# Transposes in pairs ahead of the scores: a two-layer graph-attention kernel

## The chip, the cores and the metric

The kernel runs on one core of a Trainium2 chip. A core has five engines that this text calls by short names: PE (TensorE, matrix products), DVE (VectorE), ACT (ScalarE), POOL (GpSimd) and SP (SyncE, which issues DMAs). PE multiplies with a grid of 128 x 128 cells, reads its operands from the on-chip memory SBUF and writes its results to PSUM, a small memory from which DVE or ACT must fetch them. The metric is the device time of one execution in microseconds (us).

## What is computed

The input x is 16 graphs ("batches") of 1,024 nodes with 256 features, adj a 1024 x 1024 mask for each graph. Two layers follow each other, both as `x = x + layer(relu(layernorm(x)))`. Cut to what matters:

```python
def _L0_gnn_ref(x, adj_matrix, gamma1, beta1, gamma2, beta2, W1, b1, W2, b2):   # layer 0
    normed = layer_norm(x, gamma1, beta1)
    qkv = normed.reshape(b_, n_, H, HD).transpose(0, 2, 1, 3)     # 8 heads of 32; q = k = v
    scores = jnp.einsum('bhqd,bhkd->bhqk', qkv, qkv) * scale
    attn = jax.nn.softmax(jnp.where(mask, scores, -jnp.inf), axis=-1)
    out = jnp.einsum('bhqk,bhkd->bhqd', attn, qkv)
    x = x + out.transpose(0, 2, 1, 3).reshape(b_, n_, d_)
    y = layer_norm(x, gamma2, beta2)
    return x + jax.nn.gelu(y @ W1 + b1, approximate=False) @ W2 + b2

def _L1_gnn_ref(feat, adj, W, a_1, a_2, a_12, W_1, W_2):          # layer 1
    h = feat @ W
    logits = swapaxes(h @ a_1) + h @ a_2 + (h @ a_12) @ swapaxes(h)
    e = where(adj > 0, leaky_relu(logits, 0.2), NEG_INF)
    h_prime = softmax(e) @ feat
    return elu(feat @ W_1 + h_prime @ W_2)
```

All products are in float32.

## The kernel before

**Two kinds of work share PE.** Layer 0's attention is cut into *units*: for a batch, 2 halves of the queries x 2 groups of 4 heads x 8 key tiles give 32 units. A unit (`attention`, `scores` at line 922, `weigh` at 969) computes the scores of 4 heads into PSUM (tile `s`, L937), DVE adds the mask (L958), ACT takes Exp (L961), and a unit later PE weighs the values with it (tile `o`, L974). The sums of the softmax are made by DMA: POOL issues for each key tile two transfers that add `e` to `acc` (L999), and two units after a group's end PE reduces `acc` to `den` (L888); `finish` (L901) transposes `ds` and `os` and divides.

Everything else of a batch (the MLP of layer 0 and all of layer 1) is the generator `rest` (L1054). It runs one batch behind: between two units of batch b + 1, PE does some pieces of `rest` of batch b. A batch is handled in 4 chunks of 256 nodes:

- `prepare(c)` (L1039): statistics on DVE (`norm_stats`, L699, with a power on POOL, L710), later the normalized rows y; `turn(c)` (L1085) transposes them on PE (pty, L1095), and DVE scales them into yT (L1099);
- `expand(c)` (ph, hid) and `contract(c)` (po, L1149 adds it to xb): the two products of the MLP;
- `prepare1(c)`, `turn1(c)` (L1155, L1165): normalized rows ft, transposes ptf, Relu on ACT into fT (L1174);
- `project` (puT, to uT by ACT, L1186), `values` (pg, to gw by ACT or DVE in turn, L1201), `weights` (lg, then L1219, L1224 on DVE, Exp on ACT, L1225), and `attend` (own part pf, copied to z by ACT at L1240, and pa).

The next batch's values `va` are prepared by `prologue` (L740), whose `turn(i)` (L783) transposes them for chunk i (ptk, L788) into kT.

**The order** is written out: a loop takes the generators by a number that each yields as its place, so that the pieces of `rest` are spread evenly over the units, and the instructions of each engine keep the order in which the loop issued them. A transpose is not issued where it is asked for: `ask(turn, c)` puts it in the list `turns`, and `make_turns` (L872) issues what is in it just ahead of the next unit's scores. `wait_for` lets `rest` go on only when a turn has been made. `defer(us, f)` (L723) issues f when an estimated clock has run on by so many us, or earlier if `run_deferred` forces it.

**PE's shapes.** A product of `rest` is issued as four products of 32 columns (`matmul`, L565; "128*32" in the profile), scores use 32 rows ("32*128"), and a transpose the whole grid ("128*128"). A group is four transposes of 128 x 128 into one PSUM tile.

**PSUM.** Two tiles hold the scores, one the weighed values; all else shares three tiles (pool `psm`, `ps_tile`, L558). A new tile takes the place of the one that was let go first, and PE waits until that has been read.

In a steady batch there are 16 groups of transposes ahead of scores: four each of pty, ptf and ptk, and four pairs of ptds and ptos from `finish`; a pair stands in one place and is counted once here.

Of the kernel before, what the change touches and what calls it, by code (L numbers as in the profile page):

```python
# [493 lines left out]
def fast_path(  # L494
# [63 lines left out]
    def ps_tile(shape, name, dtype=F32):  # L558
        return psm.tile(shape, dtype, tag="ps", name=name)
# [15 lines left out]
    def rows(src, b, t, cols=slice(None)):  # L575
        pair = src[b, t // 2 * 2 * P : (t // 2 + 1) * 2 * P, cols]
        return pair.rearrange("(p r) d -> p r d", r=2)[:, t % 2, :]
# [121 lines left out]
    def norm_stats(srcs, name):  # L699

        nt = len(srcs)
        st = smallp.tile([P, nt, nc.vector.BN_STATS_DIM], F32, tag="st", name=f"st_{name}")
        mv = smallp.tile([P, nt, nc.vector.BN_AGGR_DIM], F32, tag="mv", name=f"mv_{name}")
        for t in range(nt):
            nc.vector.bn_stats(st[:, t, :], srcs[t])
            nc.vector.bn_aggr(mv[:, t, :], st[:, t, :])
        ve = smallp.tile([P, nt], F32, tag="ve", name=f"ve_{name}")
        nc.vector.tensor_scalar_add(ve, mv[:, :, 1], EPS)
        rs = smallp.tile([P, nt], F32, tag="rs", name=f"rs_{name}")
        nc.gpsimd.tensor_tensor(rs, ve, mhalf[:, :nt], op=ALU.pow)  # L710
        return mv, rs

    def normalize(dst, src, mv, rs, t):
        nc.vector.tensor_scalar(
            dst, src, mv[:, t, 0:1], rs[:, t : t + 1], op0=ALU.subtract, op1=ALU.mult
        )
# [6 lines left out]
    def defer(us, f):  # L723
        deferred.append((clock[0] + us, len(deferred), f))

        return clock[0] + us
# [13 lines left out]
    def prologue(b, st):  # L740
# [42 lines left out]
        def turn(i):  # L783
            clock[0] += 0.5
            pt = ps_tile([P, NG, CW], f"ptk_{b}_{i}")
            for g in range(NG):
                for j in range(TPC):
                    nc.tensor.transpose(  # L788
                        pt[:, g, j * P : (j + 1) * P], va[:, i * TPC + j, g * P : (g + 1) * P], ident
                    )  # L790
            nc.scalar.copy(kT[:, :, i * CW : (i + 1) * CW], pt)
# [5 lines left out]
            lambda i: measure(i, "b"),  # L797
            value,
            lambda i: None,
            lambda i: turns.append((1, lambda: turn(i))),  # L800
        ]
        if b == 0:

# [64 lines left out]
    turns = []  # L868
# [170 lines left out]
    def prepare(b, st, c):  # L1039

        h = hs[b]
        assert finished[b, c // 2] == NG
        ts = range(c * TPC, (c + 1) * TPC)
        mv, rs = norm_stats([h[t // TPH][:, t % TPH, :] for t in ts], f"c{b}_{c}")

        def apply():
            y = tmpp.tile([P, TPC, D], F32, tag="y", name=f"y_{b}_{c}")
            for i, t in enumerate(ts):
                normalize(y[:, i, :], h[t // TPH][:, t % TPH, :], mv, rs, i)
            st["y", c] = y, None  # L1050

        st["y", c] = None, defer(5.0, apply)

    def rest(b, st, tails):  # L1054
# [4 lines left out]
        def load(c):  # L1059
            for t in range(c * TPC, (c + 1) * TPC):  # L1060
                xt.append(xbp.tile([P, D], F32, tag="xb", name=f"xb_{b}_{t}"))
                nc.sync.dma_start(xt[t], rows(x, b, t))


        def add_residuals(t):
            ht = h[t // TPH][:, t % TPH, :]
            nc.gpsimd.tensor_add(ht, ht, b2r)
            nc.gpsimd.tensor_add(xt[t], xt[t], ht)
# [4 lines left out]
        def ask(turn, c):  # L1073

            def f():
                clock[0] += 0.5
                turn(c)
                turned.add((turn, c))
            turns.append((1, f))

        def wait_for(turn, c):
            while (turn, c) not in turned:
                yield 0.0, None

        def turn(c):  # L1085
            if st["y", c][1] is not None:
                run_deferred(st["y", c][1])
            y = st["y", c][0]
            for i in range(TPC):
                defer(4.0 * i + 2.0, lambda t=c * TPC + i: add_residuals(t))  # L1090
            yT[c] = tmpp.tile([P, DC, CW], F32, tag="yT", name=f"yT_{b}_{c}")
            pt = ps_tile([P, DC, CW], f"pty_{b}_{c}")
            for dc in range(DC):
                for i in range(TPC):
                    nc.tensor.transpose(  # L1095
                        pt[:, dc, i * P : (i + 1) * P], y[:, i, dc * P : (dc + 1) * P], ident
                    )
            for dc in range(DC):
                nc.vector.tensor_scalar(  # L1099
                    yT[c][:, dc, :],  # L1100
                    pt[:, dc, :],
                    g2[:, dc : dc + 1],
                    be2[:, dc : dc + 1],
                    op0=ALU.mult,
                    op1=ALU.add,
                )

        def expand(c):
            yield from wait_for(turn, c)
            hid = midp.tile([P, FC, CW], F32, tag="mid", name=f"hid_{b}_{c}")  # L1110
            for f0 in range(0, FC, 2):
                ph = ps_tile([P, 2, CW], f"ph_{b}_{c}_{f0}")
                for i in range(2):
                    for dc in range(DC):
                        matmul(
                            ph[:, i, :],
                            w1[:, dc, (f0 + i) * P : (f0 + i + 1) * P],
                            yT[c][:, dc, :],
                            start=(dc == 0),
                            stop=(dc == DC - 1),  # L1120
                        )
                nc.vector.tensor_tensor(  # L1122
                    hid[:, f0 : f0 + 2, :],
                    ph,
                    b1c[:, f0 : f0 + 2].unsqueeze(2).to_broadcast([P, 2, CW]),
                    op=ALU.add,
                )
                yield 1.75, True
            return hid, defer(1.0, lambda: nc.scalar.activation(hid, hid, AF.Gelu))  # L1129

        def contract(c, hid):
            hid, ready = hid
            run_deferred(ready)
            for i in range(TPC):
                t = c * TPC + i
                po = ps_tile([P, D], f"po_{b}_{t}")
                for f in range(FC):
                    matmul(
                        po,
                        hid[:, f, i * P : (i + 1) * P],  # L1140
                        w2[:, f, :],
                        start=(f == 0),
                        stop=(f == FC - 1),
                    )
                    if f == FC // 2 - 1:
                        open_sums[0] = 1
                        yield 1.75, True
                        open_sums[0] = 0
                nc.vector.tensor_add(xt[t], po, xt[t])  # L1149
                yield 1.75, True  # L1150
# [124 lines left out]
            yield 1.75, True  # L1275

        load(0)
        ask(turn, 0)
        yield
        load(1)  # L1280
        hid = {0: (yield from expand(0))}
        ask(turn, 1)
        yield from tails[b]()
        while finished.get((b, 1), 0) < NG:
            yield 0.0, None
        prepare(b, st, 2)
        load(2)
        hid[1] = yield from expand(1)
        ask(turn, 2)
        prepare(b, st, 3)  # L1290
        yield from contract(0, hid[0])
        load(3)
        hid[2] = yield from expand(2)
        ask(turn, 3)
        prepare1(0)
        yield from contract(1, hid[1])
        hid[3] = yield from expand(3)
        prepare1(1)
        fT = st["fT"] = midp.tile([P, DC, N], F32, tag="mid", name=f"fT_{b}")
        ask(turn1, 0)  # L1300
        yield from contract(2, hid[2])
        prepare1(2)
        ask(turn1, 1)
        yield from contract(3, hid[3])
        uT = midp.tile([P, DC, N], F32, tag="mid", name=f"uT_{b}")
        prepare1(3)
        ask(turn1, 2)

        def some_values(*ts):
            for t in ts:  # L1310
                values(t, fT)
                yield 0.9, t % 2 == 1
# [5 lines left out]
        def some_weights(c, *pairs):  # L1318
            for i in pairs:
                first.append(weights(c, i))  # L1320
                yield 1.75, True
# [3 lines left out]
        yield from wait_for(turn1, 1)  # L1325
        yield from project_half(0, 0)
        yield from some_values(0, 1)
        ask(turn1, 3)
        yield from project_half(0, 1)
        yield from some_values(2, 3)  # L1330
        yield from wait_for(turn1, 2)
        yield from some_values(4, 5)
        yield from some_weights(0, 0, 1)
        yield from wait_for(turn1, 3)
        yield from project_half(1, 0)
        yield from project_half(1, 1)
        yield from some_values(6, 7)

        before = None
        for c in range(NCH):  # L1340
# [81 lines left out]
    while any(p is not None for p in places):  # L1422
        i = min((p, i) for i, p in enumerate(places) if p is not None)[1]
# [101 lines left out]
```

## Time and profile before

| | |
|---|---|
| median of 4 runs | 3539.82 us (3533.82 to 3546.57) |
| profiled execution | 3545.33 us, span of its instructions 3543.5 us |
| busy: PE, DVE, ACT, POOL | 98%, 77%, 52%, 40% of the span |
| granted clock of PE, mean | 0.997 |
| one batch, from its scores to the next batch's | some 217 us (ptf of the first chunk at 447.82, 667.02, 881.32, ... us) |
| transposes: ptk, ptds, pty, ptf, ptos | 256 instructions each, 272 to 273 ns a piece in the median |
| mask add on DVE (L958), 128 x 1024 | 1217 ns |
| Exp of scores on ACT (L961), 128 x 1024 | 1058 ns |
| acc DMAs: 864 of 512 KB | 6.0 us from issue to landing (median), the queue's packets take 69.9% of 16 DMA engines |

In the profile, a line such as `L1171 PE MATMUL ptf<-ident,ft` names the line of the code, the engine, the operation, and the tiles written and read. In lists by time the first number is the start in us from the span's start, the second the length of a run of equal instructions, and in brackets stands an idle time before it with what ended it. An end of a matmul is modelled, so costs on PE are best read from start to start. A wait "PE ptf L1171 <- DVE ft L714" means that PE's instruction writing ptf was held up until DVE had written ft.

### The profile page before, as it was taken

To read this page: it belongs to the slowest core of one execution; us is meant where nothing else is said; L and a number is where in the kernel's file an instruction comes from. 1 tells how busy PE (TensorE), PEld (TensorE's weight loads), DVE (VectorE), ACT (ScalarE), POOL (GpSimd) and SP (SyncE) were. 2 spreads that over 40 slices of the span, in tenths; PEclk is the share of its full clock that TensorE was granted. 3 is DMA by queue.
4 is the path that set the end of the run, shared out by engine and by line. 5 is a ranking of instruction groups with operands and counts; after the bars stand their busy time and mean duration, and the time that the engine had idled before them with its cause. 6 is when DMAs were issued, how large, how long until landed. Compare 5 with 4: busy or idle time off the path is not lost.

```text
span 3543.5 us, 107149 instructions
## 1 busy us (share of the span) xinstructions
PE 3455.9 (98%) x46494; PEld 1679.0 (47%) x46494; DVE 2737.4 (77%) x5189; ACT 1855.0 (52%) x2184; POOL 1417.8 (40%) x1708
## 2 busy tenths in 40 slices
PE   6999999999999999999999999999999999999998
PEld 2344444444444444444444444544444444444477
DVE  6878787787777878878887887887878777787744
ACT  5655554555555555555555555455555555555522
POOL 3543443434434344453434434344443444433220
PEclk9999999999999999999999999999999999999999
DMA  7788989999899998989999898998989989899710
GB/s 184 159 175 175 186 167 175 172 187 186 158 178 171 182 191 164 186 169 182 190 170 187 167 188 175 179 183 162 186 165 187 183 164 181 165 182 181 151 41 14
DMA packets 281859, 597.79 MB, mean 169 GB/s; under 512 B 94882, under 2 KB 130084, under 8 KB 281380
## 3 DMA queue, kind: packets, MB, share of 16 engines
q0 software_dynamic: 124416, 453.04, 69.9%
q1 hardware_dynamic: 154276, 134.41, 15.0%
q8 instruction: 367, 6.01, 0.7%
q10 hardware_dynamic: 2688, 3.41, 0.3%
q14 instruction: 112, 0.92, 0.1%
HBM read 104.21 MB, written 16.78 MB: 34 GB/s over the span
## 4 chain that ended last, share of the span: by engine, by line
PE 72%; DMA 14%; issue 5%; DVE 4%; POOL 2%; ACT 2%; ACTq 0%; SPq 0%; POOLq 0%; DVEq 0%
DMA acc<-e 13%; PE s L937 12%; PE pa L570 10%; PE o L974 10%; PE lg L570 9%; PE ph L570 8%; PE po L570 7%; PE pf L570 3%; PE pg L570 2%; PE puT L570 2%; DVE e L958 1%; PE den L888 1%; PE ptk L788 1%; PE pa L567 1%; POOL acc L999 1%
## 5 line engine op out<-in xcount | busy, mean ns | idle before, releaser
L999 POOL DMA_DIRECT2D acc<-e x864 | 762.7, 889 | 1669.0 <-DMA acc<-e 678.5
L961 ACT ACTIVATE e<-e 128x1024 f32<-128x1024 f32 x852 | 895.9, 1058 | 1011.5 <-DVE e L958 773.2
L958 DVE TENSOR_TENSOR e<-s,mk 128x1024 f32<-128x1024 f32 x852 | 1002.7, 1217 | 178.8 <-PE s L937 149.4
L937 PE MATMUL s<-kT 32*128 32x512 f32 x4096 | 595.7, 643 | 7.6 <-DVE e L958 5.3
L974 PE MATMUL o<-e,va 128*32 128x512 f32 x3456 | 463.8, 607 | 2.1 <-ACT e L961 2.1
L570 PE MATMUL lg<-fT,uT 128*32 128x256 f32 x7680 | 449.2, 380 | 0.0
L570 PE MATMUL ph<-yT,w 128*32 128x256 f32 x7808 | 447.4, 379 | 0.0
L570 PE MATMUL pa<-gw,e 128*32 128x258 f32 x7552 | 446.6, 380 | 0.0
L570 PE MATMUL po<-w,hid 128*32 128x256 f32 x7680 | 439.0, 379 | 0.0
L570 PEld LDWEIGHTS ph<-yT,w 128*32 128x32 f32 x7808 | 255.2, 110 | 212.3 <-issue 51.1
L570 PEld LDWEIGHTS lg<-fT,uT 128*32 128x32 f32 x7680 | 252.6, 110 | 209.3 <-issue 44.7
L570 PEld LDWEIGHTS po<-w,hid 128*32 128x32 f32 x7680 | 249.8, 110 | 209.4 <-issue 59.5
L570 PEld LDWEIGHTS pa<-gw,e 128*32 128x32 f32 x7552 | 244.9, 110 | 210.1 <-issue 56.9
L1219 DVE SCALAR_TENSOR_TENSOR e<-lg,gw,mk 128x256 f32<-128x256 f32 x512 | 223.2, 477 | 73.5 <-PE lg L570 63.0
L1225 ACT ACTIVATE e<-e,shift 128x512 f32<-128x512 f32 x256 | 182.1, 717 | 178.9 <-DVE e L1224 118.3
L1122 DVE TENSOR_TENSOR hid<-ph,b1c 128x512 f32<-128x512 f32 x256 | 175.2, 687 | 93.2 <-PE ph L570 77.6
L937 PEld LDWEIGHTS s<-kT 32*128 32x128 f32 x4096 | 163.8, 183 | 169.3 <-issue 114.8
L974 PEld LDWEIGHTS o<-e,va 128*32 128x32 f32 x3456 | 68.9, 108 | 331.1 <-issue 191.2
L961 ACT ACTIVATE acc<-acc 128x1024 f32<-128x1024 f32 x124 | 130.6, 1058 | 126.0 <-DVE acc L958 121.9
L1224 DVE SCALAR_TENSOR_TENSOR e<-e 128x512 f32<-128x512 f32 x256 | 189.6, 740 | 8.8
L958 DVE TENSOR_TENSOR acc<-s,mk 128x1024 f32<-128x1024 f32 x124 | 146.0, 1218 | 16.5 <-PE s L937 16.2
L1129 ACT ACTIVATE hid<-hid 128x2048 f32<-128x2048 f32 x64 | 122.4, 1912 | 37.7 <-DVE hid L1122 37.0
(144 smaller groups left out, 3827.3 us busy)
## 6 DMA issues: line engine op xcount, KB each, us to landing
acc<-e POOLq DMA_DIRECT2D x864, 512.0 KB, 6.0
adj<-in_adj_dram SPq DMA_DIRECT2D x248, 256.0 KB, 5.1
h<-in_x_dram SPq DMA_DIRECT2D x64, 256.0 KB, 6.2
xb<-in_x_dram SPq DMA_DIRECT2D x128, 128.0 KB, 5.0
out_dram<-z SPq DMA_DIRECT2D x128, 128.0 KB, 3.6
adj<-in_adj_dram SPq DMA_DIRECT2D x4, 512.0 KB, 6.7
mk<-mq SPq DMA_TRANSPOSE x128, 6.8
w<-in_L_gnn_W_dram ACTq DMA_DIRECT2D x2, 1024.0 KB
```

The costliest lines, as they stand in the source:

```text
L567: nc.tensor.matmul(out, lhsT, rhs, start=start, stop=stop)
L570: nc.tensor.matmul(out[c : c + HD], lhsT[:, c : c + HD], rhs, start=start, stop=stop)
L937: nc.tensor.matmul(sc[j // 2][:, j % 2, :], kT[r, g, kt * P : (kt + 1) * P], kT[r, g, qs], start=j >= by_pe, stop=True,)
L958: nc.vector.tensor_tensor(e, masked, mb, op=ALU.add)
L961: weights = lambda e=e, masked=masked: nc.scalar.activation(e, masked, AF.Exp, scale=SCALE)
L974: nc.tensor.matmul(o[j * HD : (j + 1) * HD, :], va[:, kt, (g * GH + j) * HD : (g * GH + j + 1) * HD], es[j // 2][:, j % 2, :], start=(kt = ...
L999: nc.gpsimd.dma_start(a, e, accum_op=ALU.add)
L1122: nc.vector.tensor_tensor(hid[:, f0 : f0 + 2, :], ph, b1c[:, f0 : f0 + 2].unsqueeze(2).to_broadcast([P, 2, CW]), op=ALU.add,)
L1129: return hid, defer(1.0, lambda: nc.scalar.activation(hid, hid, AF.Gelu))
L1219: nc.vector.scalar_tensor_tensor(e[:, j, :], lg[:, j, :], gw[:, kt, D : D + 1], st[c // 2][:, kt // 2, qs, kt % 2], op0=ALU.add, op1=ALU.add,)
L1224: nc.vector.scalar_tensor_tensor(e, e, ALPHA, e, op0=ALU.mult, op1=ALU.max)
L1225: ready = defer(2.5, lambda: nc.scalar.activation(e, e, AF.Exp, bias=shift))
```

## The change

Transposes of the same kind are asked for two at a time, so that `make_turns` issues two groups, one right behind the other, ahead of the same scores.

- `prologue` asks for the value chunks (ptk) in pairs: nothing after an even chunk, both after the odd one.
- In `rest`, the MLP's chunks 0 and 1 are turned together, before `expand(0)`, and chunks 2 and 3 together, after `expand(1)`. With them move the loads of x for chunks 1 and 3 (`load`, two DMAs each on SP), the statistics and normalization of chunk 3 (`prepare(b, st, 3)`), and the two additions for each row tile that a turn defers on POOL (`add_residuals`).
- Layer 1's chunks 0 and 1 are turned together after one of the two row tiles of `contract(2)`; the generator `half` is stepped twice before they are asked for.
- Layer 1's chunks 2 and 3 are turned together, later: after the first four `values` and both halves of `project` for the first two chunks. While they are awaited, `weights` of chunk 0 for the first two pairs of key tiles are issued, and the values of tiles 4 to 7 come after the second half's projections.

In the built program of a steady batch 10 groups stand ahead of scores instead of 16: six pairs of the above, and the four of `finish`. In all batches together the groups fall from 259 to 167. All computations, their sizes and their numbers are unchanged.

```diff
-            lambda i: turns.append((1, lambda: turn(i))),
+            lambda i: turns.extend((1, lambda k=k: turn(k)) for k in (i - 1, i) if i % 2),
...
         load(0)
+        load(1)
         ask(turn, 0)
+        ask(turn, 1)
         yield
-        load(1)
         hid = {0: (yield from expand(0))}
-        ask(turn, 1)
         yield from tails[b]()
         while finished.get((b, 1), 0) < NG:
             yield 0.0, None
         prepare(b, st, 2)
         load(2)
+        prepare(b, st, 3)
         hid[1] = yield from expand(1)
+        load(3)
         ask(turn, 2)
-        prepare(b, st, 3)
+        ask(turn, 3)
         yield from contract(0, hid[0])
-        load(3)
         hid[2] = yield from expand(2)
-        ask(turn, 3)
         prepare1(0)
         yield from contract(1, hid[1])
         hid[3] = yield from expand(3)
         prepare1(1)
         fT = st["fT"] = midp.tile([P, DC, N], F32, tag="mid", name=f"fT_{b}")
+        half = contract(2, hid[2])
+        yield next(half)
+        yield next(half)
         ask(turn1, 0)
-        yield from contract(2, hid[2])
+        ask(turn1, 1)
+        yield from half
         prepare1(2)
-        ask(turn1, 1)
         yield from contract(3, hid[3])
         uT = midp.tile([P, DC, N], F32, tag="mid", name=f"uT_{b}")
         prepare1(3)
-        ask(turn1, 2)
...
         yield from wait_for(turn1, 1)
         yield from project_half(0, 0)
         yield from some_values(0, 1)
-        ask(turn1, 3)
         yield from project_half(0, 1)
         yield from some_values(2, 3)
+        ask(turn1, 2)
+        ask(turn1, 3)
+        yield from some_weights(0, 0, 1)
         yield from wait_for(turn1, 2)
-        yield from some_values(4, 5)
-        yield from some_weights(0, 0, 1)
         yield from wait_for(turn1, 3)
         yield from project_half(1, 0)
         yield from project_half(1, 1)
-        yield from some_values(6, 7)
+        yield from some_values(4, 5, 6, 7)
```

## The prediction

> **What bounds the kernel now.** I read the page first: engines, granted clock, the chain that ended last.
>
> ```profile
> span 3543.5 us, 107149 instructions
> PE 3455.9 (98%) x46494; PEld 1679.0 (47%) x46494; DVE 2737.4 (77%) x5189; ACT 1855.0 (52%) x2184; POOL 1417.8 (40%) x1708
> PE 72%; DMA 14%; issue 5%; DVE 4%; POOL 2%; ACT 2%; ACTq 0%; SPq 0%; POOLq 0%; DVEq 0%
> ```
>
> TensorE is the bound: 98% busy, at a granted clock of 0.997 (the view of cores). Whatever leaves its queue is saved, and whatever makes it wait is paid. Next I read what it waits for, in the view of waits (us in total, times, longest):
>
> ```profile
> PE ptf L1171 <- DVE ft L714: 6.9, 8, 1.6
> PE pg L570 <- DVE xb L1149: 6.3, 4, 2.4
> PE ph L567 <- DVE yT L1099: 4.5, 3, 3.2
> PE ptos L909 <- DVE e L1219: 3.4, 14, 0.2
> PE puT L570 <- ACT gw L1201: 3.3, 5, 1.5
> ```
>
> The waits are few. Three of the five lie at transposes or just behind them (ptf, ptos, and ph behind pty), and there VectorE is late. Last I read the order in time around transposes, the first numbers being start and length:
>
> ```profile
> 1038.28 0.66 PE L909 MATMUL ptds<-ident,ds 128*128 128x128 f32 x4
> 1038.78 0.60 PE L909 MATMUL ptos<-ident,os 128*128 128x128 f32 x4
> 1039.31 1.14 PE L937 MATMUL s<-kT 32*128 32x512 f32 x8
> ...
> 1050.23 3.64 PE L570 MATMUL po<-w,hid 128*32 128x256 f32 x64
> 1053.80 0.66 PE L1095 MATMUL pty<-ident,y 128*128 128x128 f32 x4
> 1054.39 1.14 PE L937 MATMUL s<-kT 32*128 32x512 f32 x8
> ```
>
> From start to start, a lone group of four transposes (pty) keeps the scores back by 0.59 us; `finish`, which is already a pair (ptds, ptos), keeps them back by 0.50 + 0.53 = 1.02 us. So a second group behind a first costs 0.44 us, not 0.59: a pair saves 0.15 us.
>
> The same pair elsewhere shows its price, with one row of VectorE's order in time before two of TensorE's:
>
> ```profile
> 1201.95 0.87 DVE L1219 SCALAR_TENSOR_TENSOR e<-lg,gw,mk 128x256 f32<-128x256 f32 x2
> ...
> 1202.06 0.66 PE L909 MATMUL ptds<-ident,ds 128*128 128x128 f32 x4
> 1202.97 0.63 PE L909 MATMUL ptos<-ident,os 128*128 128x128 f32 x4 [0.25 <-DVE e L1219]
> ```
>
> Here ptos starts 0.91 us after ptds instead of 0.50: its PSUM tile is freed only when VectorE has read lg. That is +0.41 us in 14 of the 16 batches, more than a pair saves.
>
> **The change, part by part.** In the built program's order the matmuls between the scores stay nearly the same; groups of transposes fall from 259 to 167. Some five of the 92 lie in the last batch, where no scores follow.
>
> (a) *Pairs:* 87 x 0.15 = -13.0 us. [...]
>
> (b) *ptf_1 comes a unit earlier,* straight behind ptf_0, and needs chunk 1's normalized rows (ft, L714). These are where they were in VectorE's queue. One row of TensorE, one of VectorE:
>
> ```profile
> 1101.04 0.66 PE L1171 MATMUL ptf<-ident,ft 128*128 128x128 f32 x4
> 1102.42 0.73 DVE L714 TENSOR_SCALAR ft<-xb,mv_d,rs_d 128x256 f32<-128x256 f32 x2
> ```
>
> Over batches 0 to 14, ft_1 ends 0.08 to 2.12 us after ptf_0's start (mean 1.20). Where transposes already wait for ft they start 0.18 us before its second half ends; ptf_1 could start at +0.49. So it waits for what is over 0.67: summed over the batches, +8.5 us. Queued behind it are the unit's scores, then the mask add that waits for them, then Exp. Bounds: 0, if VectorE runs earlier, and 15 x 1.45 = 21.8 with the largest row everywhere.
>
> (c) *ptk_1 behind ptk_0,* in the unit that has just computed pf_0. Its PSUM tile is pf_0's, which ScalarE must first copy to z:
>
> ```profile
> 1156.35 0.66 PE L788 MATMUL ptk<-ident,va 128*128 128x128 f32 x4
> 1156.86 0.46 ACT L1240 ACTIVATE z<-pf,minus 128x256 f32<-128x256 f32 x1
> ```
>
> z starts 0.44 us after pf's last matmul ends in batches 1 to 13 (0.53 in batch 0), because two Exps (1.32 us) are ahead of it. It ends at 1157.32, so ptk_1 starts at about 1157.38 instead of 1156.84: 0.54 x 14 = +7.6 us. Bounds: 0.17 a batch, if z starts 0.07 us after pf as in the next-to-last batch, and 1.26 with one more Exp of 0.72 ahead; I take the row, which is the same everywhere. [...]
>
> (d) *ptf_2 and ptf_3 move behind lg_0 and lg_1.* The old waits there go: ptf_3 for ft, by start-to-start 7.5 us over eight batches; ptk_0, 0.34 x 11 = 3.8; puT, about 3.3; and of pg's 6.3 some 2.4, which (b) now waits out beforehand. Together -17.0. What is late next: ScalarE gets the Relu of ptf_3 behind the Exp of lg_1. From ft_3's end VectorE does statistics 1.28, copy 0.42, two mask adds 2.35, then for lg_0 0.88 + 0.69, normalize 0.73, for lg_1 0.88 + 0.69; ScalarE then Exp 0.72 and Relu 0.60: 9.24 us until the next puT may start (durations of the fifth batch's rows, 1128 to 1142 us). TensorE reaches puT 9.35 us after pg_3 by its rows: scores and weighing 1.95 twice, lg 3.57, the pair 1.02, den 0.86. It comes to pg_3 earlier by ptf_2's 0.59 and a pair's 0.15, less its wait in (b), so it waits where ft_3 ends more than 0.1 us after pg_3. With ft_3's end of each batch these waits sum to 8.0 us; then pg_5 waits for the copy of puT behind two Exps, 0.35 in nine batches, with some tenths in the others 3.6. Net -17.0 + 11.6 = -5.4. Bounds: -17 (nothing late), and +15 if every batch is as late as the worst (1.80 + 0.35, 15 times, 32 us, less 17).
>
> (e) *The last batch* has nothing between its parts. pty_1 moves ahead of the last score unit, and with it go 3.20 us of idling and 1.64 us of half clock (the ph group behind it took 8.83 against 7.19). pty_3 hides in pty_2's wait: 1.24 less. ptf_3's wait grows: from lg_1's end 0.07 + 0.88 + 0.69 + 0.72 + 0.60 + 0.1 = 3.1, where ptf_2 and ptf_3 with their waits took 0.49 + 0.31 + 0.60 + 0.85 = 2.3. Together -3.20 - 1.64 - 1.24 + 0.8 = -5.3 us.
>
> (f) *What costs nothing, and its cover.* Chunk 3's statistics on VectorE (1.28), its pow on POOL (0.71) and normalize (0.73) move a unit earlier, before the mask adds of the next unit: these end some 1.5 us later, at about 1051.8 (0.56 of VectorE's idling takes the rest), and the scores that need them start at 1054.4 or later. Moved up, pow passes four acc-DMA issues on POOL, the first of which starts 1.3 us later. yT_1 and yT_3 put 1.00 us each before a mask add whose next scores are 5 us off. Two x loads each pass one output store (0.34) on SP, which nobody waits for. Residual adds come four at a time on POOL, 1.05 + 0.73 us more between two acc issues at four places in a batch. The cover is the slack of the sums: the last issue at 1232.41 lands in 6.0 (median) at 1238.4, den starts at 1244.2. Without it, up to 1.8 x 60 = 107 us. A gain is not excluded either, as POOL's order changes which issue waits.
>
> *Sum:* -13.0 + 8.5 + 7.6 - 5.4 - 5.3 = -7.6 us. It is made against an execution of 3545.33 us, 5.5 above the median of the four runs, 3539.82; from the median, 3532. About 0.3% (10.6 us) is what a measurement of this kernel can tell from no change.
>
> **Rivals.** *The waits stay away:* VectorE and ScalarE move up with TensorE, (b) and (c) are worth 0. For it: ft_1 is late by 0.76 or less in six batches. Against: z's row is equal everywhere. -7.6 - 16.1 = -24, so 3516; half of it 3524.
>
> *Slower, by one queue:* the Relu of ptf_3, behind the Exp of lg_1, holds puT in every batch as in the worst, +20 us: 3552. It turns the sum at a mean wait of (11.6 + 7.6) / 15 = 1.3 us a batch in (d). For it: ft waits 54.8 us for POOL, which waits 678.5 us for acc DMAs. Against: in seven batches ft_3 ended before pg_3 did.
>
> *The DMA sums are the bound:* the queue of acc is busy 69.9% of 16 engines, and DMA holds 14% of the chain; a shorter TensorE would only wait at den: 3540. Against: den waited for it twice, 3.6 us in all.
>
> **How the numbers follow.** Forecast (-7.6, from -3 to -14) 0.42; waits stay away 0.28; DMA bound 0.12; slower 0.18. Half of the first rival's half-way house and a quarter of the forecast's own width are over 10.6 us: faster 0.28 + 0.11 = 0.39; same 0.31 + 0.12 = 0.43; slower 0.18. The likeliest case alone spans 3525 to 3537. The range cuts a tenth on each side: 3515 (the first rival nearly whole) to 3551 (nearly the slower one).
>
> **What would show it.** ptf, ptk and pty groups of eight, 1.02 us from first start to scores; a new wait of ptf for ft of some 0.6 us a batch; one of ptk for z, 0.54; the wait of ptf_3 for ft gone, and puT waiting for fT; in the last batch no 3.2 us gap. I am wrong if the pairs save less than 0.1, if POOL's adds delay den or Exp's inputs, or if a new gap brings the half clock mid-run.

## The result and the profile after

The changed kernel takes 3552.94 us in the median of 52 runs (3537.11 to 3577.42), the kernel before 3548.48 us in the median of 78 runs on the same chips (3525.98 to 3567.94). The ratio is 1.0021, with a 95% interval from 1.0011 to 1.0031: by this ratio about 7.5 us slower (the two medians alone differ by 4.5), where 7.6 us faster was forecast. The change is smaller than the 0.3% that the prediction named, but the interval leaves out "no change", the sign is the wrong one, and the median lies above the forecast range of 3515 to 3551 us. Part of that distance is the starting point: the forecast of 3532 us was counted from the median of four runs, 3539.82, and 78 runs of the same kernel have 3548.48.

The profiled executions say the opposite, 3542.93 us after against 3545.33 before. Each is one draw from runs that scatter by 40 us, so times of single profiles are not compared here; what is read from a profile is what repeats in every batch.

The page of the changed kernel, the same three lines as before:

```profile
span 3541.1 us, 107204 instructions
PE 3448.5 (97%) x46494; PEld 1680.1 (47%) x46494; DVE 2715.8 (77%) x5189; ACT 1856.6 (52%) x2184; POOL 1406.0 (40%) x1708
PE 78%; DVE 8%; DMA 6%; issue 4%; ACT 2%; POOL 1%; ACTq 0%; SPq 0%; DVEq 0%; POOLq 0%
```

TensorE is busy for 7.4 us less, and is still the bound. The view of waits (total, times, longest) shows what came in their place:

```profile
PE ptf L1171 <- DVE ft L714: 9.5, 13, 1.4
...
PE ptk L788 <- ACT z L1240: 7.1, 14, 0.6
...
PE den L888 <- DMA acc<-e: 4.9, 2, 3.6
PE ptos L909 <- DVE e L1219: 3.4, 14, 0.2
PE ptf L1171 <- DVE e L1219: 3.2, 5, 1.1
PE pg L570 <- DVE xb L1149: 3.2, 2, 1.9
PE ptos L909 <- DVE hid L1122: 3.1, 4, 1.4
PE puT L567 <- ACT fT L1174: 2.9, 2, 2.1
PE puT L570 <- ACT fT L1174: 2.9, 6, 0.5
...
PE pty L1095 <- DVE y L714: 1.6, 1, 1.6
```

The waits for ft, formerly at ptf_3, now stand at ptf_1. The one for z is new and equal in 14 batches. `ph` behind `pty` (4.5 us) is nearly gone. The last line is one that the prediction did not have.

TensorE's order in time around three pairs (start, length of the run of equal instructions, idle time before it with its releaser in brackets):

```profile
1098.19 0.66 PE L1171 MATMUL ptf<-ident,ft 128*128 128x128 f32 x4
1099.43 0.67 PE L1171 MATMUL ptf<-ident,ft 128*128 128x128 f32 x4 [0.58 <-DVE ft L714]
1100.03 1.14 PE L937 MATMUL s<-kT 32*128 32x512 f32 x8
...
1153.44 0.66 PE L788 MATMUL ptk<-ident,va 128*128 128x128 f32 x4
1154.60 0.63 PE L788 MATMUL ptk<-ident,va 128*128 128x128 f32 x4 [0.50 <-ACT z L1240]
1155.16 1.14 PE L937 MATMUL s<-kT 32*128 32x512 f32 x8
...
1174.37 1.09 PE L788 MATMUL ptk<-ident,va 128*128 128x128 f32 x8
1175.40 1.14 PE L937 MATMUL s<-kT 32*128 32x512 f32 x8
```

The last pair, value chunks 2 and 3, waits for nothing and holds the scores for 1.03 us. The pair of value chunks 0 and 1 holds them for 1.72 us (1153.44 to 1155.16) and that of layer 1's first chunks for 1.84. Two lone groups would take 1.17. So a pair gains 0.15 us where both its tiles and both its inputs are there, and in the rows above loses 0.55 and 0.67 us where one is not.

### The profile page after: what moved, and what is told of

It is laid out like the page before. It is cut to its first block, busy times and chain, and to the rows that moved or that the text cites. A ratio compares the mean times of both kernels' runs of the same rounds, so it can differ in the third digit from the quotient of the medians.

```text
span 3541.1 us, 107204 instructions
## 1 busy us (share of the span) xinstructions
PE 3448.5 (97%) x46494; PEld 1680.1 (47%) x46494; DVE 2715.8 (77%) x5189; ACT 1856.6 (52%) x2184; POOL 1406.0 (40%) x1708
## 4 chain that ended last, share of the span: by engine, by line
PE 78%; DVE 8%; DMA 6%; issue 4%; ACT 2%; POOL 1%; ACTq 0%; SPq 0%; DVEq 0%; POOLq 0%
PE s L937 13%; PE pa L570 12%; PE o L974 11%; PE ph L570 10%; PE lg L570 8%; PE po L570 8%; DMA acc<-e 5%; PE pg L570 3%; PE puT L570 3%; PE pf L570 3%; DVE e L958 2%; PE den L888 1%; PE pa L567 1%; PE pty L1095 1%; DVE e L1219 1%
## 5 line engine op out<-in xcount | busy, mean ns | idle before, releaser
L999 POOL DMA_DIRECT2D acc<-e x864 | 754.9, 881 | 1655.7 <-ACT e L961 732.5
```

Source lines behind the costliest of these rows:

```text
L999: nc.gpsimd.dma_start(a, e, accum_op=ALU.add)
```

## The experiments

**First theory, "waits":** the pairs save what they should, and the waits at ptf_1 and ptk_1 take it back. **Rival, "POOL":** the loss comes from the residual additions that now stand four at a time between the acc DMAs. The ratios below are against the kernel before.

*ptf01_late.* Layer 1's first pair one unit later:

```diff
-        half = contract(2, hid[2])
-        yield next(half)
-        yield next(half)
-        ask(turn1, 0)
-        ask(turn1, 1)
-        yield from half
+        yield from contract(2, hid[2])
         prepare1(2)
+        ask(turn1, 0)
+        ask(turn1, 1)
```

> Layer 1's chunks 0 and 1 are still turned as a pair, but one unit later. Theory 'waits' (a pair saves 0.15 us, and the change loses by waits at two pairs): the wait of ptf for ft, 12.9 us over the run in the changed kernel's trace, goes, and the changed kernel's +7.4 us against the kernel before becomes -5.5 us, ratio 0.9985; ptf groups of eight fall from 1.58 us in the median to 1.02 for the first pair of a batch. Theory 'POOL' (the loss comes from the residual additions that stand four at a time between the acc DMAs): nothing of that is touched, the ratio stays at 1.0021.

Measured: 3552.05 us, ratio 1.001 (0.9983 to 1.0038). The first pair now takes 1.02 us from its start to the scores in every batch, so that wait did go. But in the same trace the second pair (ptf_2, ptf_3) takes 1.38 us in the median, and den, ahead of puT, 1.52 instead of 0.86: TensorE waits there for the Relu of ptf_3 (puT for fT, 4.8 us in ten waits). The interval holds the numbers of both theories.

*ptk23_only.* Value chunks 0 and 1 singly again, 2 and 3 as a pair:

```diff
-            ... for k in (i - 1, i) if i % 2),
+            ... for k in {0: (0,), 1: (1,), 2: (), 3: (2, 3)}[i]),
```

> Value chunks 0 and 1 are turned singly as in the kernel before, chunks 2 and 3 as a pair. Theory 'waits': 9.8 us of waiting for z go, 15 lone groups come back at 0.15 us, +2.2: together -7.6, so from +7.4 to about 0, ratio 1.0000. Theory 'POOL': the waits are replaced by others, only the +2.2 us shows, ratio 1.0027.

Measured: 3556.48 us, ratio 1.0021 (0.9999 to 1.0043). Again the interval holds both numbers, 1.0000 and 1.0027.

*both_undone.* The two edits together.

> Both edits at once: chunks 0 and 1 of layer 1 as a pair one unit later, value chunks 0 and 1 singly. Theory 'waits': 12.9 + 7.6 = 20.5 us less than the changed kernel, so -13 us against the kernel before, ratio 0.9963, faster than both. Theory 'POOL': ratio 1.0021 to 1.0027.

Measured: 3558.77 us, ratio 1.0023 (1.0002 to 1.0044). The 13 us did not come: 0.9963 lies outside the interval. Four of TensorE's waits in this kernel:

```profile
PE pg L570 <- DVE xb L1149: 9.7, 7, 2.0
...
PE ptf L1171 <- DVE e L1219: 8.4, 11, 1.8
PE ptk L788 <- ACT uT L1186: 7.1, 13, 0.6
PE puT L570 <- ACT fT L1174: 5.7, 12, 0.5
```

The waits for ft and for z are gone, and others of 5.7 to 9.7 us stand at four places (that of pg for xb stood in the kernel before too). The wait for z has a twin: where ptk_0 stands alone in its old place, its PSUM tile is now one of puT's, which ScalarE has not yet copied to uT. So the first theory falls in this form: undoing a wait at its place does not give its time back.

*mlp_only.* The kernel before with the MLP's pairs alone:

```diff
         load(0)
+        load(1)
         ask(turn, 0)
+        ask(turn, 1)
...
         load(2)
+        prepare(b, st, 3)
         hid[1] = yield from expand(1)
+        load(3)
         ask(turn, 2)
-        prepare(b, st, 3)
+        ask(turn, 3)
...
```

> The kernel before with the MLP's chunks turned in pairs and nothing else: 31 pairs, the residual additions four at a time, the loads and chunk 3's statistics earlier. Theory 'waits': 31 x 0.15 = -4.7, the last batch's gap and half clock -5, ptos behind hid +3: about -7 us, ratio 0.998. Theory 'POOL': here is all of the loss and only a third of the gain, so +10 us or more, ratio 1.003.

Measured: 3550.95 us, ratio 1.0006 (0.9987 to 1.0024). Neither number: the interval leaves out both, 0.998 and 1.003.

**Second theory, "DMA":** where a wait comes from lateness that the acc DMAs make (in the trace of *both_undone* POOL's issues of them wait 679.9 us for earlier ones, VectorE's ft waits 70.4 us for POOL's powers, and its mask adds 22.9 us for tiles that an acc DMA still reads), it can't be removed at its place. A piece of the order in time of *both_undone* shows such a chain, across VectorE, POOL and TensorE:

```profile
2634.76 1.23 DVE L958 TENSOR_TENSOR e<-s,mk 128x1024 f32<-128x1024 f32 x1 [2.04 <-DMA acc<-e]
2635.18 0.92 POOL L999 DMA_DIRECT2D acc<-e  x1 [3.07 <-DMA acc<-e]
...
2638.91 1.01 POOL L710 TENSOR_TENSOR rs_d<-ve_d,mhalf 128x2 f32<-128x2 f32 x1
...
2639.95 0.74 DVE L714 TENSOR_SCALAR ft<-xb,mv_d,rs_d 128x256 f32<-128x256 f32 x2 [3.64 <-POOL rs_d L710]
...
2643.52 0.41 DVE L1149 TENSOR_TENSOR xb<-po,xb 128x256 f32<-128x256 f32 x1
...
2643.98 1.08 PE L570 MATMUL pg<-wo,fT 128*32 128x258 f32 x16 [1.49 <-DVE xb L1149]
```

**Rival, "engines":** the order of work on the engines alone makes the difference. To tell these apart, both kernels ran without the acc DMAs.

```diff
-            for e, a in zip(es, sums[g, qh]):
-                nc.gpsimd.dma_start(a, e, accum_op=ALU.add)
+            return
...
+    great = const.tile([P, 1], F32, name="great")
+    nc.gpsimd.memset(great, 1e9)
...
-        nc.scalar.copy(ds, den)
+        nc.scalar.activation(ds, den, AF.Identity, bias=great, scale=0.0)
```

> The kernel before without the 864 acc DMAs: the sums of layer 0's softmax are left out, and the copy of den writes a constant in their place; all else is issued as before. Theory 'DMA' (the acc DMAs are late, POOL and VectorE wait for them in order, and TensorE waits for these): VectorE's waits for acc DMAs and the stalls of pg, ptf and pty behind them go; of the 80 us by which TensorE's groups exceed their shortest, some 40 go, and the steady batch (median 214.7 us) falls to about 212. Theory 'engines' (the waits come from the order of work on VectorE and ScalarE): less than 10 us goes.

> The changed kernel without the 864 acc DMAs, with the same omission. Theory 'DMA': the pairs' gain shows against the kernel before without them: -13 us, -5 in the last batch, +9.8 for the wait for z, which no DMA stands behind: about -8 us, from -4 to -14. Theory 'engines': the same +5 to +7 us against it as with the DMAs.

Measured: 3496.99 us (3496.25 to 3502.32, 6 runs) for the kernel before, ratio 0.9849 (0.9822 to 0.9875), and 3504.93 us (3503.30 to 3508.49) for the changed one. Of TensorE's waits in *noacc_before* the three that the prediction's part (d) counted on are not in the view any more (ptf for ft, pg for xb, puT for gw, 6.9, 6.3 and 3.3 us with the DMAs); a steady batch falls from 214.7 to 212.8 us, and nearly all of them take the same to 0.1 us. So "DMA" is right about the waits of the kernel before. But a difference of the same size stays: +7.9 us against +7.5. "POOL" is not needed for it, as no acc DMA is left; the gain that "DMA" expected of the changed kernel did not come, and "engines" holds for these two kernels. That the loss with the acc DMAs has the same parts is not shown by this.

What the DMAs make is some 50 us in both kernels, and most of the scatter: the standard deviation is 9.0 us in the 78 runs of the kernel before, 2.9 in these six. The six fall into two clusters some 5 us apart (granted clock 0.996 in the two long runs, 0.998 to 0.999 in the other four), and the profiled run of *noacc_before*, 3501.99 us, is a long one. So a difference of a few us between the medians of such kernels is weak by itself; the steady batch, the same to 0.1 us from batch to batch, is the better measure. It was also the same on another chip: *noacc_first_single*, below, has the steady batch of *noacc_after* in the same order, and there too it takes 213.1 us.

That gave a way to see a few microseconds. The waits of *noacc_after*, a view with few lines left (up to the omitted lines this kernel's numbers are 2 higher than the changed kernel's, behind them 1 higher):

```profile
PE ptk L790 <- ACT z L1241: 7.1, 14, 0.5
PE ptos L911 <- DVE e L1220: 3.4, 14, 0.2
PE puT L567 <- ACT fT L1175: 2.9, 2, 2.1
PE pty L1096 <- DVE y L716: 2.8, 1, 2.8
```

From start to start, a steady batch differs from that of *noacc_before* at these places: six pairs, -0.90 us; ptf_1 0.16 late for ft; den and pg behind the second ptf pair together +0.35; ptk_1 +0.69 for z. That is +0.30, and the batches take 213.1 against 212.8. Outside the steady batches, batch 0 takes 153.1 against 148.5 us (from the first den to the fifth), and all that follows the 61st den 298.8 against 302.0.

Batch 0 was not in the prediction. In *noacc_after*, VectorE and TensorE:

```profile
144.76 0.66 PE L1096 MATMUL pty<-ident,y 128*128 128x128 f32 x4
...
147.72 0.72 DVE L716 TENSOR_SCALAR y<-h,mv_c,rs_c 128x256 f32<-128x256 f32 x2
148.17 1.22 PE L1096 MATMUL pty<-ident,y 128*128 128x128 f32 x4 [2.75 <-DVE y L716]
...
150.30 2.09 PE L939 MATMUL s<-kT 32*128 32x512 f32 x8
```

pty_1 is asked for with pty_0, its rows y are normalized 3 us later, and the instructions after the wait are slow: eight scores take 2.09 us instead of 1.14. The windows of 129 to 149 and 149 to 170 us show granted clocks of 0.97 and 0.87.

*first_single.* The repair of this, first with the acc DMAs:

```diff
         ask(turn, 0)
-        ask(turn, 1)
+        if b:
+            ask(turn, 1)
         yield
         hid = {0: (yield from expand(0))}
+        if not b:
+            ask(turn, 1)
```

> The changed kernel, but in batch 0 alone the MLP's chunk 1 is turned after chunk 0's first product, as before; all other pairs stay. In the changed kernels' traces the stretch of batch 0 from its third to its fourth den takes 39 to 40 us against 34.1 in the one trace before, behind a wait of pty for y of 1.6 to 2.5 us and a granted clock of 0.87 after it. If the pair makes that: 5 us less than the changed kernel, ratio 1.0007, and the stretch falls to 34 us. If that stretch only varies from run to run: no difference, 1.0021.

Measured: 3553.98 us, ratio 1.0001 (0.9981 to 1.0022), and the stretch took 40.9 us. Inconclusive: pty's wait for y is gone, but in this execution VectorE waited 3.60 us for a load of adj just before, the scores 2.54 us for VectorE, and the clock fell to 0.84 there.

*before_again.* The kernel before, a second profile.

> The kernel before, profiled a second time. If the short stretch in batch 0 belongs to the kernel, it is 34 us again, and pg waits for xb and pty's scores for e in the same batches; if the traces differ by chance, it lies between 34 and 40 and the stalls lie elsewhere.

Measured: 3554.06 us; the stretch took 36.8 us, with a wait of the scores of 1.89 us. So that stretch varies also in the kernel before, and with the DMAs a single trace can't settle it. Without them it can:

*noacc_first_single.* The same edit on *noacc_after*.

> The changed kernel without the acc DMAs (omission as in noacc_after), and in batch 0 alone the MLP's chunk 1 is turned after chunk 0's first product, as before. If the pair in batch 0 costs what the two traces without acc DMAs show (148.5 against 153.1 us for batch 0): 4.6 us less than noacc_after's 3504.93, so 3500.3. If that is one execution's chance: 3504.9 again.

Measured: 3499.48 us (3497.34 to 3501.37), 5.4 less than *noacc_after*. The pair in batch 0 costs 5 us. The other traces without acc DMAs, here and below, agree: batch 0 takes 151.7 to 153.1 us in the three kernels that have this pair and 146.0 to 148.5 in the four that don't.

*noacc_held.* The pair of value chunks 0 and 1 one unit later, behind pa_0 instead of pf_0:

```diff
-            lambda i: turns.extend((1, ...
+            lambda i: (held if i == 1 else turns).extend((1, ...
...
             room -= n
             f()
+        turns.extend(held)
+        held.clear()
```

> The changed kernel without the acc DMAs, the pair of value chunks 0 and 1 held back by one unit, so that it no longer stands right behind pf_0. If ptk's wait is for the PSUM tile of pf_0, which ScalarE must copy to z: it goes, 14 x 0.69 = 9.7 us less than 3504.93, so 3495. If any place takes two of three tiles from somebody who is late: another wait of the same size, 3505.

Measured: 3495.25 us (3493.64 to 3498.21), 9.7 less. The steady batch falls from 213.1 to 212.4 us, the wait for z is gone, and little took its place (scores wait for `e` 1.0 us longer in all). So the wait is one for pf_0's tile, and it costs what its rows say.

*noacc_mlp_only.* The MLP's pairs alone.

> The kernel before without the acc DMAs, the MLP's chunks in pairs and nothing else. By the traces without acc DMAs: 31 pairs x 0.15 = -4.7, the last batch -3.2, batch 0 +4.6: -3.3 from noacc_before's 3496.99, so 3493.7. If the pairs saved nothing: -3.2 + 4.6, so 3498.4.

Measured: 3494.51 us (3493.70 to 3494.69), 2.5 less than *noacc_before*. In the trace the steady batch takes 212.5 us instead of 212.8: two pairs, 0.15 us each. All that follows the 61st den takes 295.7 us instead of 302.0, so 6.3 less, where the expectation had booked 3.2; that its total came out within 1 us is in part luck.

*first_single_held.* Both repairs, with the acc DMAs.

> With the acc DMAs and all sums: both repairs together, batch 0's chunk 1 turned singly, the pair of value chunks 0 and 1 one unit later. If the sums without acc DMAs carry over: -4.6 - 9.7 from the changed kernel's +7.4, so -7 us against the kernel before, ratio 0.998. If stalls behind late acc DMAs take up what the pairs and the repairs save: +7, ratio 1.002.

Measured: 3549.45 us, ratio 0.9995 (0.9969 to 1.0020). It lies between the two; the interval holds both -7 us and the +7 that is the other theory's, the latter at its end.

*noacc_ptf23_only.* What was open now was part (d), the pair of ptf_2 and ptf_3 behind lg_0 and lg_1. Alone on the kernel before, without the acc DMAs:

```diff
-        ask(turn1, 2)
...
-        ask(turn1, 3)
         yield from project_half(0, 1)
         yield from some_values(2, 3)
+        ask(turn1, 2)
+        ask(turn1, 3)
+        yield from some_weights(0, 0, 1)
         yield from wait_for(turn1, 2)
-        yield from some_values(4, 5)
-        yield from some_weights(0, 0, 1)
         yield from wait_for(turn1, 3)
         yield from project_half(1, 0)
         yield from project_half(1, 1)
-        yield from some_values(6, 7)
+        yield from some_values(4, 5, 6, 7)
```

> The kernel before without the acc DMAs, and of the change only the last part: ptf_2 and ptf_3 as a pair behind lg_0 and lg_1, the values of tiles 4 to 7 after the projections. If this part loses by what comes behind it (puT waits for the Relu of ptf_3, pg for puT's copy), and has no old waits to remove where acc DMAs are missing: -0.15 for the pair and +0.38 in 14 batches, +3 us, so 3500. If it were the gain that the prediction made it (-17 + 11.6 and the pair's 2.1): 3489.

Measured: 3514.92 us (3512.72 to 3516.48), 17.9 more than *noacc_before*. Worse than either: the waits show one that I had not seen.

```profile
PE ptk L790 <- ACT uT L1187: 7.9, 14, 0.6
...
PE puT L567 <- ACT fT L1175: 2.9, 2, 2.1
```

The first is the twin met in *both_undone*: with this part alone, ptk_0 stands right behind puT and pg. It fits that undoing the pair of value chunks gained nothing there. The second is in the last batch. The order in time there, *noacc_before* first, then *noacc_after*:

```profile
3422.64 0.60 PE L1172 MATMUL ptf<-ident,ft 128*128 128x128 f32 x4
3424.09 3.70 PE L567 MATMUL puT<-fT,wm 128*128 128x512 f32 x8 [0.85 <-ACT fT L1175]
3427.63 1.91 PE L567 MATMUL pg<-wo,fT 128*128 128x258 f32 x8
```

```profile
3423.94 1.04 PE L1172 MATMUL ptf<-ident,ft 128*128 128x128 f32 x8
3427.10 5.40 PE L567 MATMUL puT<-fT,wm 128*128 128x512 f32 x8 [2.13 <-ACT fT L1175]
3432.34 3.65 PE L567 MATMUL pg<-wo,fT 128*128 128x258 f32 x16
```

From ptf to pg it is 4.99 against 8.40 us: the longer wait, and puT after it 1.70 us slower. The wait recurs in every kernel that has this pair, the slow puT does not. *noacc_first_single*:

```profile
3420.51 3.70 PE L567 MATMUL puT<-fT,wm 128*128 128x512 f32 x8 [2.12 <-ACT fT L1175]
```

From start to start these eight puT take 5.2 us in four of the ten traces with this wait and 3.5 in six, the changed kernel's among the six. The steady batches (213.6 against 212.8 us in thirteen of them) and the 3.4 us of the last batch make 13.8 of the 17.9 us; the two profiled spans differ by 14.5.

*noacc_four_pairs* and *four_pairs.* If the sum of causes is complete, pairs that nobody is late for must give the whole gain. This kernel has the MLP's pairs (batch 0's first two singly), the value pairs with the first one held a unit, layer 1's first pair one unit later, and ptf_2 and ptf_3 singly as before. Its edits are those of *mlp_only*, *first_single* and *noacc_held*, and this one against the kernel before:

```diff
-        ask(turn1, 0)
         yield from contract(2, hid[2])
         prepare1(2)
+        ask(turn1, 0)
         ask(turn1, 1)
```

> Without the acc DMAs: the kernel before with four kinds of pairs where no tile is late: the MLP's (batch 0's first two chunks singly), the value chunks' (the first pair held back by one unit), and layer 1's chunks 0 and 1 one unit later; ptf_2 and ptf_3 as before. If pairs save 0.15 us each and these have no wait: 75 x 0.15 = -11.3 and -2.4 in the last batch, -13.7 from 3496.99, so 3483. If new waits come with these too: 3490 or more.

> The same kernel with the acc DMAs and all sums. If the gain carries over: -13.7, ratio 0.9961, faster than both kernels. If TensorE only arrives earlier where acc DMAs are late: half of it or less, ratio 0.998 to 1.000.

Measured: 3484.03 us (3483.59 to 3484.65) without the acc DMAs, 13.0 less than *noacc_before*, and its steady batch takes 212.0 us, 0.75 less: five pairs, 0.15 us each. (What follows the 61st den is 6.4 us shorter in the trace, where 2.4 were booked for the last batch; so here too the agreement of the totals is in part luck.) With the acc DMAs it takes 3536.34 us against 3550.69 for the kernel before on the same chip: ratio 0.9967 (0.9951 to 0.9982). That is some 12 us faster than the kernel before. It was not timed beside the changed kernel, but the two intervals against the kernel before don't touch. The waits for xb and ft are still there:

```profile
PE pg L570 <- DVE xb L1152: 11.8, 6, 2.6
...
PE ptf L1174 <- DVE ft L714: 6.9, 8, 1.6
```

In the kernel before they were 6.3 and 6.9 us, in its second profile 9.2 and 7.7. They go with the DMAs, as *noacc_before* showed, and the pairs gain beside them.

## Why the prediction was wrong, by its own steps

**(a) Pairs, -13.0:** right. A pair that waits for nothing takes 1.02 us from its start to the scores, and without the acc DMAs the steady batch is 0.30 us shorter with two such pairs and 0.75 with five.

**(b) ptf_1 waits for ft, +8.5:** the wait came, 9.5 us in the view of waits and 12.9 from start to start, of which 0.16 us a batch remains without the acc DMAs. Right in kind, and somewhat too small.

**(c) ptk_1 waits for z, +7.6:** right in kind; the term was 9.7, as *noacc_held* measured by taking it away. In the changed kernel's order in time z starts at 1154.00 and takes 0.46, and ptk_1 starts at 1154.60, 0.14 us after z's end and not 0.06; the pair took 1.72 us instead of 1.56.

**(d) ptf_2 and ptf_3, -17.0 + 11.6 = -5.4:** the step that failed most. The old waits for ft, xb and gw were booked as removed because the instructions they stood at move. They are lateness behind the acc DMAs: without those DMAs they are not in the view, and what the move itself makes is a loss, 0.35 us in each of thirteen steady batches (+4.6 us where -5.4 was booked) inside the changed kernel, and 17.9 us when it is done alone.

With the DMAs, compare each trace with that of the same order without them, over batches 0 to 13. The stretch from a batch's first puT to its next ptds, where (d) works, is 24 and 29 us longer in the two traces of the kernel before, 32 in *mlp_only*, 34 in *four_pairs*; it is 8, 21 and 18 us longer in the changed kernel, *first_single* and *first_single_held*, and 24 to 29 in the three other kernels with (d). The rest of these batches is 10 to 16 us longer in the four traces without (d), and 17, 21 and 20 in the changed kernel, *first_single* and *first_single_held*. So some lateness left the stretch and some came back in the rest: 38 to 47 us in all against 25 to 42. Whether (d) taken alone gains or loses with the DMAs is not settled by traces that scatter this much.

**(e) The last batch, -5.3:** the MLP's half came, -6.3 in the trace of *noacc_mlp_only* for the -6.1 of its three terms, but 1.64 of it was chance: in *before_again* the same wait of 3.20 us was not followed by a slow ph group (6.98 us from start to start, 8.67 in the first profile). The ptf pair's +0.8 was mis-sized: +3.4 measured where the slow puT follows the wait, some 1.5 where it does not. In *noacc_after*, where it does, -3.2 in all.

**(f) What costs nothing:** failed at one place. The MLP's pair was costed for steady batches, and batch 0, where y is not ready for a second group, stood in the sum at nothing, without a reason: +4.6 to 5.4 us, as *noacc_first_single* measured by taking it away. For the rest of it, POOL and the DMAs, nothing speaks against the cover: a loss of the same size is there without the acc DMAs.

With these numbers, in the kernels without acc DMAs, -13.0 + 2.1 + 9.7 + 4.6 - 3.2 + 4.6 = +4.8 us, where the two spans differ by 6.5 and the medians by 7.9. Against the forecast's terms that is -6.4 in (b), +2.1 in (c), +10.0 in (d), +2.1 in (e) and +4.6 in (f). By stages the two traces differ by +0.5 us ahead of the first den, +4.6 in batch 0, +4.4 in the next fourteen batches and -3.2 behind; some 2 us of that are in none of the terms. That the loss with the DMAs has the same size, +7.5, was measured; that there the larger wait at ptf_1 and the lateness that left (d)'s stretch about cancel is argued from the traces, not shown apart.

**Rivals.** "Slower, by one queue" named 3552, and the median is 3552.94, but that is luck: it was counted from a base 8.7 us lower, and its mechanism is only a part, as puT's wait for the Relu is 2.9 us in six batches, not 20. "The waits stay away" is refuted by the waits for z. "The DMA sums are the bound" is half right: they cost both kernels some 50 us, yet a shorter TensorE is not swallowed by them, as *four_pairs* shows.

## What to carry to other kernels

A wait in a profile belongs to whoever is late, not to the place where it is seen (here 20.5 us of waits, undone at their places in *both_undone*, left the ratio at 1.0023). Before a move is credited with removing one, ask what made it late, and whether it will not be just as late for the next in the queue. When two groups are put together, check for each pair which PSUM tile the second takes and who still reads it (here pf_0's, at 0.69 us a batch), and look at the first and the last batch by themselves: a wait there costs itself and sometimes slow matmuls behind it (here 2.75 us in batch 0 of *noacc_after*, then eight scores in 2.09 us instead of 1.14, with a granted clock of 0.87 over the 21 us that hold them). If a kernel's scatter hides the effect, find what makes the scatter and take it out of both versions; here that turned a difference of 0.2% into one that can be placed batch by batch.

## What was not expected of the hardware

- Most of the scatter between runs comes with the accumulating DMAs: 17 runs of the kernel before on one chip lay between 3537.86 and 3570.18 us, and without these DMAs four runs of *noacc_mlp_only* between 3493.70 and 3494.69.
- Idling of 2.1 to 2.8 us in the middle of dense work was followed by slow matmuls, but not each time. Behind 2.75 us in batch 0 eight scores took 2.09 us instead of 1.14 in all three traces without acc DMAs that have this wait; behind 2.1 us in the last batch eight puT took 5.2 us from start to start in four traces and 3.5 in six. Even 3.20 us there had no slow ph behind it in *before_again*. Waits of 0.5 to 0.6 us, as at ptk_1 and ptf_1, had no such effect: the scores behind them take 1.14.
- Without the acc DMAs four of five expected totals were met to about 1 us: *noacc_first_single*, *noacc_held*, *noacc_mlp_only* and *noacc_four_pairs* came out at 3499.5, 3495.3, 3494.5 and 3484.0 where 3500.3, 3495, 3493.7 and 3483 were expected, two of them partly by luck, as said above. *noacc_ptf23_only* missed by 15.
